# Two attention blocks in one kernel: the second product of layer 0 is copied out of PSUM unscaled and scaled on GpSimd, the prologue is rebuilt, and norms and weight sums are pinned in the instruction order

## The chip, the cores and the metric

One NeuronCore of a Trainium2 chip runs the kernel in a single launch. The metric is the device time in microseconds (us) of one execution. TensorE (PE) does the matrix products, VectorE (DVE), ScalarE (ACT) and GpSimd (POOL) the elementwise work, and SyncE (SP) issues nearly all DMAs. All arithmetic is in float32.

## The reference

Eight images of 512 channels by 32x32 pixels (T = 1024 tokens) pass through two attention layers. Layer 0 has eight heads of 64 channels, layer 1 one head of 512.

```
h   = group_norm(x, 32 groups)                       # layer 0
q, k, v = w_qkv @ h + b_qkv                          # 8 heads, 64 channels each
x   = x + w_proj @ (v softmax(q^T k / 8)) + b_proj
h   = group_norm(x, 8 groups)                        # layer 1
q, k, v = q_w @ h + q_b, k_w @ h + k_b, v_w @ h + v_b
x   = x + p_w @ (v softmax(q^T k / sqrt(512))) + p_b
```

## The kernel before

**Tiling.** An image is four tiles of 128 channels by 1024 tokens (KC = 4). A half is HT = 512 tokens. All 512x512 products of weights and images are done by a Winograd-Strassen scheme with seven half-size products (`wino`, steps 1, 2, 5, 6, 7, 4, 3), so each weight needs three sums and a difference of its quarters (`left_sums`, four VectorE instructions of 128x512 each for a weight in `prepare`, L155 to L158), and each image tile likewise (`right_sums`, L166 to L169). The weight sums are made once, stored in DRAM by `keep`, and read back by `load_weight` for every later image into one of three `wpool` buffers.

**Layer 1 is folded.** Instead of q and k the kernel uses one product matrix m (from the q and k weights), and instead of v and the projection one product matrix z. They are computed on the core in the prologue: `raw` loads a weight, `natural` transposes it on TensorE and copies it out of PSUM, `product` multiplies. `bias_product` multiplies a weight with a bias vector: `ubias` (natural k weight times bq1), `obias[1]` (raw p times bv1, plus bp1) and `obias[0]` (layer 0's projection times bv0, plus bp0). It does this with the weight as the stationary operand and the vector as a moving operand of one column: 16 matmuls for each bias, and a small VectorE instruction per four of them.

**The prologue** in order: load k, q (layer 1), image 0 and the layer 0 weights; transposes of k and q; statistics of image 0; weight sums of v; product m; group mean; `ubias`; the affine terms of the norm; the norm applied to image 0 (two tiles on ScalarE, two on GpSimd); then v, q, k of image 0 by Winograd; the mean of image 1's norm; transposes of v; product z; `obias[1]`, `obias[0]`. After that the loop over the images starts.

**The skewed loop.** For each image b: `attention0(b)`, then the m-product and scores of image b-1's layer 1 and the projection of b's layer 0, the rest of layer 1 of b-1, and q, k, v of b+1.

**`attention0`** is eight blocks (pair of heads hp by token half tb). In each, eight score tiles `sc` go through ScalarE's exponential (L414), VectorE adds the eight results into `sum` (L416, L418), TensorE forms `av` from the exponentials, then `sums` (the column sums of `sum`), of which VectorE takes reciprocals (L378). The reciprocals travel through a DRAM tile `rows` and come back broadcast as `r`. `scaled` multiplies `av` in PSUM by `r` into the result `a` on VectorE (L436); it is called in the next block, between its scores and its `av`. `av` and `sums` share two PSUM buffers (`acc`), the scores have three double ones. `extra` is a list of work given out twice in each block, after the scores and after `av`: in the first image the later weights' sums, in all of them the four `norm.apply` of the next image, on ScalarE (L136).

**Order.** A planner in the framework orders the instructions of each engine by its own estimates. `tc.keep_in_program_order(i)` puts instruction i behind the instruction that was traced just before it on the same engine; what is not so marked may be moved. Before the change only TensorE's instructions are marked. An engine works through its queue in order, so an instruction that waits holds back all behind it on that engine.

Of the kernel before, what the change touches and what calls it, by code (L numbers as in the profile page):

```python
# [15 lines left out]
P = 128  # L16
# [12 lines left out]
def two_attention_blocks_kernel(  # L29
# [35 lines left out]
    def matmul(*args, **kw):  # L65
        tc.keep_in_program_order(nc.tensor.matmul(*args, **kw))  # L66

    def transpose(*args):
        tc.keep_in_program_order(nc.tensor.transpose(*args))
# [5 lines left out]
    def pcol(name, c):  # L75
        return pcols(name)[:, c : c + 1]
# [9 lines left out]


    class GroupNorm:
        def __init__(self, layer, uid):
            self.layer, self.uid = layer, uid  # L90
            self.mv = small.tile([P, KC, 2], F32, tag="mv", name=f"mv_{uid}")
            self.st = [None] * KC

        def half_stats(self, c, half, xh):
            if self.st[c] is None:
                self.st[c] = small.tile([P, 2, 6], F32, tag="bnst", bufs=8, name=f"bnst_{self.uid}_{c}")
            nc.vector.bn_stats(self.st[c][:, half, :], xh)

        def end_stats(self, c):
            nc.vector.bn_aggr(self.mv[:, c, :], self.st[c])  # L100
# [32 lines left out]
        def apply(self, engine, dst, src, c):  # L133
            s, b = self.s[:, c : c + 1], self.b[:, c : c + 1]
            if engine is nc.scalar:
                nc.scalar.activation(dst, src, AF.Identity, bias=b, scale=s)  # L136
            else:
                engine.tensor_scalar(dst, src, s, b, ALU.mult, ALU.add)

# [32 lines left out]
    def main_path(ctx):  # L172
# [14 lines left out]
        def acc_tile(name):  # L187
            return ps_acc.tile([P, HT], F32, tag="acc", name=name)
# [96 lines left out]
        def keep(n, t):  # L285
            nc.sync.dma_start(wdram[n], t)
# [108 lines left out]

        def attention0(b, q, k, v, extra):
            a = channel_tiles(f"a0_{b}")
            scaled = None
            n = 0
            for hp in range(KC):  # L400
                for tb in range(2):
                    uid = f"0_{b}_{hp}_{tb}"
                    total = pair_tile(f"sum_{uid}")
                    es = []
                    for s in range(NS):
                        sc = ps_pools[n % 3].tile([P, 2, HT], F32, tag="sc", name=f"sc_{uid}_{s}")
                        n += 1
                        for j in range(2):
                            matmul(
                                sc[:, j, :], k[hp][ts(j, 64), ts(s, P)], q[hp][ts(j, 64), ts(tb, HT)],  # L410
                                start=True, stop=True,
                            )
                        e = pair_tile(f"e_{uid}_{s}")
                        nc.scalar.activation(e, sc, AF.Exp, scale=(C // 8) ** -0.5)  # L414
                        if s == 1:
                            nc.vector.tensor_add(total, es[0], e)  # L416
                        elif s > 1:
                            nc.vector.tensor_add(total, total, e)  # L418
# [12 lines left out]
                    for f in extra.pop(0) if extra else ():  # L431
                        f()
                    r = reciprocals(total, uid, False)

                    def scaled(hp=hp, tb=tb, av=av, r=r):
                        nc.vector.tensor_mul(a[hp][:, ts(tb, HT)], av, r)  # L436

            assert not extra
            return a, scaled
# [72 lines left out]

        def raw(n, i):
            ts_ = [pair_tile(f"raw{n}_{h}") for h in range(2)]
            for h in range(2):
                nc.sync.dma_start(ts_[h], w[i, ts(h, C // 2), :].rearrange("(kc p) o -> p kc o", p=P))
            return [ts_[kc // 2][:, kc % 2, :] for kc in range(KC)]


        def natural(wt, nm):  # L520
            ts_ = [pair_tile(f"nat{nm}_{h}") for h in range(2)]
            t = [ts_[o // 2][:, o % 2, :] for o in range(KC)]
            for o in range(KC):
                pt = acc_tile(f"tr_w{nm}_{o}")
                for kc in range(KC):
                    transpose(pt[:, ts(kc, P)], wt[kc][:, ts(o, P)], ident)
                if o % 2 == 0:
                    nc.vector.tensor_copy(t[o], pt)
                else:
                    nc.scalar.copy(t[o], pt)  # L530
            return t

        def product(lhs, rhs, nm):
            ts_ = [pair_tile(f"prod{nm}_{h}") for h in range(2)]
            for ic in range(KC):
                ps = acc_tile(f"ps_w{nm}_{ic}")
                for kc in range(KC):
                    matmul(ps, lhs[kc][:, ts(ic, P)], rhs[kc], start=(kc == 0), stop=(kc == KC - 1))
                nc.scalar.copy(ts_[ic // 2][:, ic % 2, :], ps)
            for h in range(2):  # L540
                nc.sync.dma_start(products[nm][ts(h, C // 2), :].rearrange("(kc p) o -> p kc o", p=P), ts_[h])

        def bias_product(dst, lhs, vec, add, nm):
            for oc in range(KC):
                ps = acc_tile(f"ps_b{nm}_{oc}")
                for kc in range(KC):
                    matmul(
                        ps[:, 0:1], lhs[kc][:, ts(oc, P)], pcol(vec, kc), start=(kc == 0), stop=(kc == KC - 1)
                    )
                if add is None:  # L550
                    nc.vector.tensor_copy(dst[:, oc : oc + 1], ps[:, 0:1])
                else:
                    nc.vector.tensor_add(dst[:, oc : oc + 1], ps[:, 0:1], pcol(add, oc))

        def prologue():
            raw_k = raw("k", 5)
            raw_q = raw("q", 4)
            h0 = [load_x(0, c, "h0") for c in range(KC)]
            first = {n: prepare(n) for n in "vqk"}
            wk = natural(raw_k, "k")  # L560
            wq = natural(raw_q, "q")
            norm = GroupNorm(0, "0_0")
            for c in range(KC):
                norm.stats(c, h0[c])
            for f in first["v"][1]:
# [5 lines left out]
            for c in range(KC):  # L571
                norm.apply(nc.scalar if c % 2 else nc.gpsimd, h0[c], h0[c], c)
            raw_v = raw("v", 6)
            raw_p = raw("p", 7)
            hf, steps = image_factors(h0, "h0_0")
            background.extend(steps)
            for n in "qk":
                background.extend(first[n][1])
# [21 lines left out]
            return v, q, k, norm1, later  # L600

        psum_pools("first", 2)
# [360 lines left out]
```

## Time and profile before

| what | value |
|---|---|
| median of 3 timed executions | 2979.69 us (2978.97 to 2979.95) |
| span of the profiled execution | 2980.3 us |
| TensorE busy | 2942.8 us, 99% |
| VectorE busy | 1833.3 us, 62% |
| ScalarE busy | 775.2 us, 26% |
| GpSimd busy | 96.8 us, 3% |
| mean granted TensorE clock | 0.995 |

A line of a group or timeline gives the engine, the line of code, the operation, the tiles written and read, the shapes, and how often; in brackets the idle time of the engine before it and what ended it. All TensorE instructions carry the line of the helper that records them (L66 for matmuls, L69 for transposes), so tiles tell them apart: `ps_wm` and `ps_wz` are the two products, `ps_bu` and `ps_bo` the bias products, `tr_w*` the transposes, `psa_`, `psb_`, `psc_` the Winograd steps. A full float32 matmul of 512 columns shows as two records. The prologue takes 146.5 us of the span; the loop the rest.

### The profile page before, as it was taken

Reading aid. Unit: us, or ns where it says so; the run is one execution under the profiler, and the core shown is the slowest. Engines: PE = TensorE matmul, PEld = TensorE weight load, DVE = VectorE, ACT = ScalarE, POOL = GpSimd, SP = SyncE. Lnnn points to the kernel's source line nnn. Section 1 sums busy time; section 2 is a strip of 40 time slices with the busy share of each in tenths; the row PEclk is TensorE's granted clock in tenths of the full one; section 3 lists DMA queues with packets and bytes.
Section 4 is the critical chain, followed back from the end, with each engine's and each line's share of the span. In section 5 each row is a group of like instructions: output and inputs, shape, how many; then the busy total and the mean of one; then the engine's idle time right before and its main releaser. Section 6 shows DMA issues by size and latency. Waiting matters only on the chain.

```text
span 2980.3 us, 26641 instructions
## 1 busy us (share of the span) xinstructions
PE 2942.8 (99%) x10322; PEld 1408.1 (47%) x10322; DVE 1833.3 (62%) x2443; ACT 775.2 (26%) x941; POOL 96.8 (3%) x105
## 2 busy tenths in 40 slices
PE   7999999999999999999999999999999999999999
PEld 5533533555345453454534545345443455334545
DVE  4377577644776557755577645765467653676555
ACT  1153142112521134111351203411044111531110
POOL 0000000000000000000000000000000000000000
PEclk9999999999999999999999999999999999999999
DMA  6422301132011320223202222122211222112201
GB/s 260 168 80 77 150 16 66 53 145 103 19 64 54 144 106 19 90 79 114 85 20 108 96 74 85 47 82 96 92 71 47 78 103 92 40 43 78 85 7 65
DMA packets 67925, 245.78 MB, mean 82 GB/s; under 512 B 8208, under 2 KB 15184, under 8 KB 61264
## 3 DMA queue, kind: packets, MB, share of 16 engines
q1 hardware_dynamic: 67376, 243.86, 22.4%
q8 instruction: 83, 1.36, 0.2%
q14 instruction: 50, 0.41, 0.0%
q10 hardware_dynamic: 416, 0.16, 0.0%
HBM read 197.03 MB, written 46.96 MB: 82 GB/s over the span
## 4 chain that ended last, share of the span: by engine, by line
PE 85%; DVE 6%; issue 3%; DMA 3%; ACT 2%; SPq 0%; POOL 0%; DVEq 0%; ACTq 0%; POOLq 0%
PE sc L66 9%; PE av L66 9%; PE psb_sc L66 6%; PE psb_av L66 6%; DVE sum L418 5%; PE psa_av L66 4%; PE psa_sc L66 4%; PE psc_av L66 4%; PE psc_sc L66 4%; PE psb_v L66 3%; PE psb_z L66 3%; PE psb_k L66 3%; PE psb_q L66 3%; PE psb_p L66 3%; PE psb_g L66 3%
## 5 line engine op out<-in xcount | busy, mean ns | idle before, releaser
L414 ACT ACTIVATE e<-sc 128x1024 f32<-128x1024 f32 x512 | 477.0, 1049 | 490.2 <-PE sc L66 490.2
L418 DVE TENSOR_TENSOR sum<-sum,e 128x1024 f32<-128x1024 f32 x384 | 470.0, 1224 | 35.9 <-ACT e L414 1.7
L66 PE MATMUL sc<-q,k 64*128 64x512 f32 x2048 | 462.9, 601 | 4.5 <-ACT e L414 4.5
L66 PE MATMUL av<-e,v 128*64 128x512 f32 x2048 | 453.6, 595 | 0.0
L66 PEld LDWEIGHTS sc<-q,k 64*128 64x128 f32 x2048 | 190.0, 187 | 249.8 <-ACT e L414 126.7
L66 PEld LDWEIGHTS av<-e,v 128*64 128x64 f32 x2048 | 141.4, 137 | 304.3 <-issue 285.4
L378 DVE RECIPROCAL rc<-sums 128x256 f32<-128x256 f32 x72 | 126.5, 1756 | 87.3 <-PE sums L66 52.6
L416 DVE TENSOR_TENSOR sum<-e,e 128x1024 f32<-128x1024 f32 x64 | 78.4, 1226 | 69.6 <-ACT e L414 69.6
L465 ACT ACTIVATE e<-e 128x512 f32<-128x512 f32 x96 | 60.6, 631 | 232.2 <-DVE e L464 232.2
L66 PE MATMUL psa_sc<-g,h 128*128 128x512 f32 x256 | 115.7, 594 | 0.0
L66 PE MATMUL psa_av<-e,z 128*128 128x512 f32 x256 | 113.3, 595 | 0.0
L380 POOL TENSOR_TENSOR all_recs<-all_recs,rc 128x256 f32<-128x256 f32 x72 | 64.3, 892 | 1465.2 <-DVE rc L378 1450.7
L136 ACT ACTIVATE h<-h,b,s 128x1024 f32<-128x1024 f32 x62 | 76.4, 1240 | 74.4 <-DMA h<-in_x 51.1
L436 DVE TENSOR_TENSOR a<-av,r 128x512 f32<-128x512 f32 x64 | 44.0, 688 | 62.7 <-DMA r<-rows 62.5
L66 PEld LDWEIGHTS psa_sc<-g,h 128*128 128x128 f32 x256 | 48.1, 190 | 57.9 <-issue 56.2
L66 PEld LDWEIGHTS psa_av<-e,z 128*128 128x128 f32 x256 | 48.0, 190 | 57.3 <-issue 55.9
L245 ACT COPY t_sc<-psa_sc 128x512 f32<-128x512 f32 x32 | 18.7, 586 | 181.7 <-DVE x L640 152.4
L66 PE MATMUL psb_sc<-g,h 128*128 128x512 f32 x128 | 58.1, 597 | 0.0
L66 PE MATMUL psa_z<-w_z,h 128*128 128x256 f32 x256 | 57.9, 379 | 0.0
L66 PE MATMUL psb_z<-w_z,t_h 128*128 128x256 f32 x256 | 57.9, 379 | 0.0
L66 PE MATMUL psa_p<-a,w_p 128*128 128x512 f32 x128 | 57.5, 592 | 0.0
L66 PE MATMUL psb_p<-t_a,w_p 128*128 128x512 f32 x128 | 57.5, 592 | 0.0
(274 smaller groups left out, 3951.5 us busy)
## 6 DMA issues: line engine op xcount, KB each, us to landing
x<-in_x SPq DMA_DIRECT2D x36, 512.0 KB
h<-in_x SPq DMA_DIRECT2D x32, 512.0 KB
r<-rows SPq DMA_DIRECT2D x128, 128.0 KB
spill<-x SPq DMA_DIRECT2D x32, 512.0 KB
h<-spill SPq DMA_DIRECT2D x32, 512.0 KB
x<-spill SPq DMA_DIRECT2D x32, 512.0 KB
out<-x SPq DMA_DIRECT2D x64, 256.0 KB
w_p<-sums_p SPq DMA_DIRECT2D x8, 1792.0 KB
```

The source lines that it names most:

```text
L66: tc.keep_in_program_order(nc.tensor.matmul(*args, **kw))
L136: nc.scalar.activation(dst, src, AF.Identity, bias=b, scale=s)
L245: nc.scalar.copy(t1[i], ps["a", i])
L378: nc.vector.reciprocal(rc, sums)
L380: nc.gpsimd.tensor_tensor(all_recs, all_recs, rc, ALU.add)
L414: nc.scalar.activation(e, sc, AF.Exp, scale=(C // 8) ** -0.5)
L416: nc.vector.tensor_add(total, es[0], e)
L418: nc.vector.tensor_add(total, total, e)
L436: nc.vector.tensor_mul(a[hp][:, ts(tb, HT)], av, r)
L465: nc.scalar.activation(dst, dst, AF.Exp, scale=scale)
```

## The change

It has five parts.

1. **`attention0`**: after `av`, ScalarE copies it unscaled from PSUM to `a`. The multiplication by `r` then runs in place on GpSimd, for all blocks but the last of an image; for that one `scaled` still does it on VectorE, now from SBUF.
2. **Front of the prologue**: `raw` loads in four DMAs of 256 KB instead of two of 512 KB; `natural` transposes into four PSUM buffers of several pools, chunk by chunk in the order of loading, and copies afterwards, VectorE and ScalarE in turn, pinned; the statistics of image 0 are pinned behind those copies; `product` uses the PSUM pool "a" and takes hooks, by which the group mean goes in after matmul 6 of product m, and the affine terms and the norm of image 0 after matmul 9. The weight sums of v come after product m.
3. **`bias_products`**: the three bias vectors are the stationary operand (one column), the weights the moving one (512 columns), three outputs in three row groups of one PSUM bank. The rows are copied to SBUF, sent to DRAM, read back as columns, and added in the first image's attention.
4. **The four sums of each weight in `prepare`** are pinned on VectorE: for p, m, z they stay in blocks 0, 1, 2 of the first image's attention.
5. **`norm.apply` on ScalarE** is pinned.

The core of the diff:

```diff
@@ GroupNorm
-            nc.vector.bn_stats(self.st[c][:, half, :], xh)
+            stats = nc.vector.bn_stats(self.st[c][:, half, :], xh)
+            if self.pinned:
+                tc.keep_in_program_order(stats)
-                nc.scalar.activation(dst, src, AF.Identity, bias=b, scale=s)
+                tc.keep_in_program_order(nc.scalar.activation(dst, src, AF.Identity, bias=b, scale=s))
@@ prepare
-                nc.vector.tensor_add, nc.vector.tensor_sub,
+                lambda *a: tc.keep_in_program_order(nc.vector.tensor_add(*a)),
+                lambda *a: tc.keep_in_program_order(nc.vector.tensor_sub(*a)),
@@ attention0
-                    if scaled:
-                        scaled()
...
+                    dst = a[hp][:, ts(tb, HT)]
+                    nc.scalar.copy(dst, av)
                     r = reciprocals(total, uid, False)
-                    def scaled(hp=hp, tb=tb, av=av, r=r):
-                        nc.vector.tensor_mul(a[hp][:, ts(tb, HT)], av, r)
+                    if (hp, tb) != (KC - 1, 1):
+                        nc.gpsimd.tensor_tensor(dst, dst, r, ALU.mult)
+                    else:
+                        scaled = lambda dst=dst, r=r: nc.vector.tensor_mul(dst, dst, r)
@@ natural
+            pt = [ps_tile(banks[o // 2], f"tr_w{nm}_{o}") for o in range(KC)]
+            for kc in range(KC):
+                for o in range(KC):
+                    transpose(pt[o][:, ts(kc, P)], wt[kc][:, ts(o, P)], ident)
+            spread(lambda o, copy: tc.keep_in_program_order(copy(t[o], pt[o])), KC)
@@ bias_products
+            for kc in range(KC):
+                for i, (m, vec) in enumerate(lhs):
+                    matmul(ps[32 * i : 32 * i + 1, :], pcol(vec, kc), m[kc], start=(kc == 0), stop=(kc == KC - 1))
...
+            nc.sync.dma_start(rows, row[0 : 32 * n : 32, :C])
...
+                nc.sync.dma_start(cols[:, i, :], rows[i].rearrange("(c p) -> p c", p=P))
@@ prologue
-            product(wq, wk, "m")
-            norm.group_mean(acc_tile("gmean_0_0")[:, :KC])
-            bias_product(ubias, wk, "bq1", None, "u")
-            norm.affine(acc_tile("gvar_0_0")[:, :KC])
...
+            product(
+                wq, wk, "m", {6: lambda: norm.group_mean(acc_tile("gmean_0_0")[:, :KC]), 9: normed},
+            )
...
-            product(natural(raw_v, "v"), raw_p, "z")
-            bias_product(obias[1], raw_p, "bv1", "bp1", "o")
-            bias_product(obias[0], raw("p0", 3), "bv0", "bp0", "o0")
+            raw_p0 = raw("p0", 3)
+            wv = natural(raw_v, "v", "bc")
+            product(wv, raw_p, "z")
+            bias = bias_products([(wk, "bq1"), (raw_p, "bv1"), (raw_p0, "bv0")])
...
+            later.append([
+                lambda: tc.keep_in_program_order(nc.vector.tensor_copy(ubias, bias[0])),
+                lambda: tc.keep_in_program_order(nc.vector.tensor_add(obias[1], bias[1], pcols("bp1"))),
+                lambda: tc.keep_in_program_order(nc.vector.tensor_add(obias[0], bias[2], pcols("bp0"))),
+            ])
```

More of the change, by code (lines that the diff above doesn't have):

```diff
@@ L88, in two_attention_blocks_kernel, with __init__ @@
     class GroupNorm:
-        def __init__(self, layer, uid):
-            self.layer, self.uid = layer, uid
+        def __init__(self, layer, uid, pinned=False):
+            self.layer, self.uid, self.pinned = layer, uid, pinned
             self.mv = small.tile([P, KC, 2], F32, tag="mv", name=f"mv_{uid}")
@@ L397, in attention0 @@
             a = channel_tiles(f"a0_{b}")
-            scaled = None
             n = 0
@@ L514, in raw, with ps_tile @@
             ts_ = [pair_tile(f"raw{n}_{h}") for h in range(2)]
-            for h in range(2):
-                nc.sync.dma_start(ts_[h], w[i, ts(h, C // 2), :].rearrange("(kc p) o -> p kc o", p=P))
+            for kc in range(KC):
+                nc.sync.dma_start(ts_[kc // 2][:, kc % 2, :], w[i, ts(kc, P), :])
             return [ts_[kc // 2][:, kc % 2, :] for kc in range(KC)]
-        def natural(wt, nm):
+        def ps_tile(n, name):
+            return acc_tile(name) if n == "acc" else ps_pools["abc".index(n)].tile([P, HT], F32, tag="ps", name=name)
@@ L521, in natural, with spread @@
+        def spread(f, n):
+            for i in range(n):
+                f(i, nc.scalar.copy if i % 2 else nc.vector.tensor_copy)
+        def natural(wt, nm, banks):
             ts_ = [pair_tile(f"nat{nm}_{h}") for h in range(2)]
             t = [ts_[o // 2][:, o % 2, :] for o in range(KC)]
[L523 to L530, printed above, removed]
@@ L531, in natural, with product @@
-            return t
-        def product(lhs, rhs, nm):
+            pt = [ps_tile(banks[o // 2], f"tr_w{nm}_{o}") for o in range(KC)]
[3 more added lines that the diff above has]
+            spread(lambda o, copy: tc.keep_in_program_order(copy(t[o], pt[o])), KC)
+            return t
+        def product(lhs, rhs, nm, hooks=()):
+            hooks = dict(hooks)
             ts_ = [pair_tile(f"prod{nm}_{h}") for h in range(2)]
@@ L535, in product @@
             for ic in range(KC):
-                ps = acc_tile(f"ps_w{nm}_{ic}")
+                ps = ps_tile("a", f"ps_w{nm}_{ic}")
                 for kc in range(KC):
                     matmul(ps, lhs[kc][:, ts(ic, P)], rhs[kc], start=(kc == 0), stop=(kc == KC - 1))
+                    if ic * KC + kc in hooks:
+                        hooks[ic * KC + kc]()
                 nc.scalar.copy(ts_[ic // 2][:, ic % 2, :], ps)
-            for h in range(2):
-                nc.sync.dma_start(products[nm][ts(h, C // 2), :].rearrange("(kc p) o -> p kc o", p=P), ts_[h])
@@ L543, in bias_product @@
[L543 to L548, printed above, removed]
-                    )
[L550 to L553, printed above, removed]
+                if ic % 2:
+                    nc.sync.dma_start(
+                        products[nm][ts(ic // 2, C // 2), :].rearrange("(kc p) o -> p kc o", p=P), ts_[ic // 2]
+                    )
@@ new lines, in bias_products @@
+        def bias_products(lhs):
+            n = len(lhs)
+            ps = acc_tile("ps_bias")
+            for kc in range(KC):
+                for i, (m, vec) in enumerate(lhs):
+                    matmul(ps[32 * i : 32 * i + 1, :], pcol(vec, kc), m[kc], start=(kc == 0), stop=(kc == KC - 1))
+            row = big_tile("bias_rows")
+            rows = dram.tile([n, C], F32, name="bias_rows_dram")
+            for i in range(n):
+                nc.vector.tensor_copy(row[32 * i : 32 * i + 1, :C], ps[32 * i : 32 * i + 1, :])
+            nc.sync.dma_start(rows, row[0 : 32 * n : 32, :C])
+            cols = const.tile([P, n, KC], F32, name="bias_cols")
+            for i in range(n):
+                nc.sync.dma_start(cols[:, i, :], rows[i].rearrange("(c p) -> p c", p=P))
+            return [cols[:, i, :] for i in range(n)]
@@ L559, in prologue, with normed @@
             first = {n: prepare(n) for n in "vqk"}
-            wk = natural(raw_k, "k")
-            wq = natural(raw_q, "q")
-            norm = GroupNorm(0, "0_0")
+            wk = natural(raw_k, "k", ("a", "b"))
+            wq = natural(raw_q, "q", ("c", "acc"))
+            norm = GroupNorm(0, "0_0", pinned=True)
             for c in range(KC):
                 norm.stats(c, h0[c])
+            hf, steps = image_factors(h0, "h0_0")
+            def normed():
+                norm.affine(acc_tile("gvar_0_0")[:, :KC])
+                for c in range(KC):
+                    norm.apply(nc.scalar if c % 2 else nc.gpsimd, h0[c], h0[c], c)
+            product(
+                wq, wk, "m", {6: lambda: norm.group_mean(acc_tile("gmean_0_0")[:, :KC]), 9: normed},
+            )
+            raw_v = raw("v", 6)
+            raw_p = raw("p", 7)
             for f in first["v"][1]:
                 f()
-            product(wq, wk, "m")
-            norm.group_mean(acc_tile("gmean_0_0")[:, :KC])
-            bias_product(ubias, wk, "bq1", None, "u")
-            norm.affine(acc_tile("gvar_0_0")[:, :KC])
[L571 to L575, printed above, removed]
             background.extend(steps)
```

## The prediction

> **What bounds the kernel now.** First the page's busy table: TensorE is busy 99% of the span, so only three things can move the end: TensorE's idle time, work that TensorE need not do, and time at a low clock. I then asked for all of TensorE's waits.
>
> ```profile
> PE sums L66 <- DVE sum L418: 10.1, 23, 1.4
> PE tr_wk L69 <- DMA rawk<-in_w: 5.9, 2, 5.0
> PE sc L66 <- ACT e L414: 4.5, 7, 0.7
> PE tr_wk L69 <- DVE natk L528: 4.4, 1, 4.4
> PE psa_v L66 <- POOL h L138: 3.3, 1, 3.3
> ```
>
> (columns: us in total, times, longest). In the loop TensorE waits only at `sums` and `sc`: 14.6 us. Everything else is in the prologue, which TensorE's timeline shows next.
>
> ```profile
> 4.99 0.66 PE L69 MATMUL tr_wk<-ident,rawk 128*128 128x128 f32 x2 [4.99 <-DMA rawk<-in_w]
> 12.49 1.97 PE L69 MATMUL tr_wk<-ident,rawk 128*128 128x128 f32 x8 [4.36 <-DVE natk L528]
> 16.94 1.10 PE L69 MATMUL tr_wq<-ident,rawq 128*128 128x128 f32 x8 [0.68 <-ACT natq L530]
> ...
> 119.20 14.00 PE L66 MATMUL ps_wz<-rawp,natv 128*128 128x512 f32 x32
> 133.57 1.05 PE L66 MATMUL ps_bo<-par,rawp 128*128 128x1 f32 x8 [0.26 <-DVE ve L123]
> 134.93 11.60 PE L66 MATMUL ps_bo<-par,rawp 128*128 128x1 f32 x56 [0.31 <-DVE obias L553]
> 146.47 10.15 PE L66 MATMUL sc<-q,k 64*128 64x512 f32 x32
> ```
>
> Two things to see. One-column matmuls of `obias` hold TensorE from 133.57 to 146.47, 12.9 us. And the first block's scores take 10.15 us where every later block's take 7.14. The windows around them say why (after the stretch: its length, busy time and count of PE, PEld, DVE, ACT and POOL, the granted clock, the DMA share and GB/s):
>
> ```profile
> 136.00:146.00 10.00, 10.00 (x49) 10.00 (x48) 0.95 (x6) 2.45 (x2) 0.00 (x0) 0.50 1.04 393
> 146.00:152.00 6.00, 6.00 (x17) 2.90 (x19) 3.26 (x6) 2.67 (x3) 0.00 (x0) 0.50 1.00 425
> 152.00:156.00 4.00, 4.00 (x18) 1.60 (x18) 3.08 (x3) 4.00 (x5) 0.00 (x0) 0.93 0.95 407
> ```
>
> The clock is halved some 2.2 us after the one-column matmuls begin and is back only at about 152.3. The same happens once earlier: `ubias` and the wait for the norm halve it at 36.5, until 46.6, into v's first steps.
>
> **What the Trainium skill says.** (1) "TensorE: Matmul & The Clock Gate", What's actually happening: an idle window of about 3.4 us halves the array's clock, a busy one restores it. The trace agrees, with one addition: dense one-column matmuls are treated like idleness. (2) "TensorEngine Tiling (Array Packing)", Theoretical Speedup: stationary operands of at most 32 columns run up to four at a time. Agreed: `sums`, four matmuls in four column groups, takes 0.57 us from its start to the next `sc`, where one after another would be 4 x 0.43 = 1.7. (3) "SBUF — State Buffer", Who interferes with whom: a VectorE instruction with two SBUF inputs and a GpSimd instruction that reads SBUF exclude each other for the whole instruction. The trace fits: while GpSimd normed a tile (L138, 1.70 us instead of 1.20) VectorE's `t_h` took 1.52 us instead of 0.69. (4) Price: "GPSIMD Engine Reference", Elementwise: a two-input add of 2048 columns 4.50 us, so an estimate of 1.1 us for 512.
>
> **The front of the prologue (part 2).** Now v's first matmul is at 40.82. The transposes stop after six of k because VectorE, in order, sits on the statistics until image data lands (10.35), and its copy of `natk` comes behind them at 11.79. After: each engine has both copies in order before any statistics, and four PSUM buffers per weight, so transposes follow the loads. k's 1 MB had landed by 6.58; at the 0.40 to 0.43 MB per us of the next windows q's 1 MB lands about 9.1. Last four transposes 1.0 us (eight took 1.97), then on each engine two copies in a row, 0.69 each on VectorE, of which the first matmuls need one and the third and fourth the other: product m starts about 11.3 instead of 18.39. It runs 14.0, plus 0.3 for two small mean matmuls: end 25.6. The norm must keep up: statistics from 11.6, eight of 0.64 and four of 0.20, are done by about 17.3 (image tile 3 lands by about 14.3); matmul 6 ends at 11.3 + 7 x 0.86 = 17.3, so no more than 0.5 of wait; the mean's four small VectorE steps 0.8; matmul 9 at about 20.3; ve to b, on the trace 37.59 to 39.46, is 1.9: 22.3; the first tiles from GpSimd and ScalarE 1.25 later, 23.6. This lies beside the product. v then needs only the copies out of pool "a", the last two behind the norms on ScalarE: 0.6. v starts at about 26.3, **14.5 us earlier** (bounds 10 to 16.5). `ubias`'s 4.3 us on TensorE are in this sum. VectorE's weight sums of v (4 x 0.69 from 22.3) and the image sums (8 x 0.69) end before 33, where step 5 of v needs them (26.3 + 6.9). More SP issues (8 loads for 4, about 0.48 each) put q's last issue at 4.6, before its data could land; image and weight loads shift by 2 us within a DMA stream that is full anyhow. The weight sums of q, k come later than at 21 to 26, but are needed after 50.
>
> Without a pause before v the clock stays up: 40.8 to 46.6 at half speed is **2.9 us** saved (0 to 2.9).
>
> **From k to the first attention (part 3).** After: group mean as now; 16 transposes (2.0), up to 0.7 of wait for the last read of `psc_k` (117.0), first copy 0.69: product z starts at 119.5 instead of 119.2 in old time, ends with the variance matmul at 133.6. Then 12 matmuls of 512 columns, 0.86 each alone; in three column groups four rounds of 0.86, 3.6 with the fill. Neither width 1 nor this packing is in the trace: from below 3.4, from above 12 x 0.86 = 10.3 (no overlap). I take 3.6, since `sums` packs. End 137.2 instead of 146.47: **9.3 us** (2.6 to 9.5). Rows, the DRAM trip and its 4-byte columns: nothing, since the biases are first read at the projection, over 100 us later; the three tiny adds sit in block 3's VectorE slack.
>
> The 512-column stream should count as busy, and 3.6 us is short: the clock stays, the first block takes 7.1 instead of 10.1: **3.0 us** (0 to 3.0).
>
> **Attention (parts 1, 4, 5).** In a quiet block VectorE's adds end before `sums` is due; in one out of two or three the multiplication waits for `r` in VectorE's queue and the adds behind it are late:
>
> ```profile
> 403.00 0.69 DVE L436 TENSOR_TENSOR a<-av,r 128x512 f32<-128x512 f32 x1 [1.89 <-DMA r<-rows]
> 403.61 6.53 DVE L418 TENSOR_TENSOR sum<-sum,e 128x1024 f32<-128x1024 f32 x5
> 410.96 1.76 DVE L378 RECIPROCAL rc<-sums 128x256 f32<-128x256 f32 x1 [0.82 <-PE sums L66]
> ```
>
> That queue wait leaves VectorE for GpSimd, which has nothing behind it but `all_recs`. VectorE's block is then 9.2 (adds, first start to last end) after a first start 3.2 behind the scores' start: done at 12.4 of the 14.1 at which `sums` is due, 1.7 us free. GpSimd's multiplication excludes VectorE's adds for 1.1 (price above) up to 1.8 (twice `all_recs`, 0.89 for half the columns, of which some is waiting). The lower value fits into 1.7 and I take it; the upper leaves 0.1 per block, 6 us in all. ScalarE's copy (0.59 as `natk`) comes at the end of `av`, when ScalarE idles about 7 us; the next exponential is due 1.4 later, the PSUM buffer 7.6 later: nothing. The pinned norms go behind a block's exponentials, where ScalarE is idle; that removes the 0.65 us at the start of seven attentions (TensorE at `sc` behind an early L136). The pinned weight sums, 2.76 in each of blocks 0 to 2 of the first image, follow the adds and delay the reciprocal by about 1.2, of which the next block's first add feels 0.4; their stores and reloads are due at 250 or later. Of the 14.6 us I count **12.5** (0 to 14.6; below nothing is the last rival).
>
> **Sum.** 14.5 + 2.9 + 9.3 + 3.0 + 12.5 = 42.2; span 2980.3 - 42.2 = 2938.1. The timed median is 0.6 below the profiled span: 2937.5, so **2938**.
>
> **Rivals.** *A, the bias matmuls do not overlap or look idle to the clock gate*: 6.7 us more, or 3.0, or both: 2941 to 2948. For it: one-column operands did trip the gate. Against: they were the moving ones. *B, the VectorE/GpSimd exclusion eats the attention gain*: adds late by about 0.2 in most blocks, 12 us: about 2950. For: the stretched L138. Against: 1.7 us of slack. *C, the front stays bound by loads and statistics*: v at 30 to 31, clock dip kept: 2945. *D, slower*: same mechanism as B, but GpSimd holds the port longer. Prologue and `sc` gains are 34.2; over 63 blocks a wait of 0.54 each on top of the present 0.16 (10.1 / 63) undoes them, so GpSimd would have to hold VectorE off for 1.7 + 0.7 = 2.4 us per block; at 3.0 us it is 2980 + 63 x 0.6 = 3018. Against: it is twice the price.
>
> **Chances.** Likeliest 0.60, A 0.14, B 0.10, C 0.11, D 0.05. Likeliest's own range is 2931 to 2944; with A, C and most of B the range is 2930 to 2951. Less than 0.2% (6 us) can't be told from no change: faster 0.93, same 0.02, slower 0.05.
>
> **What would show it.** Product m starting near 11, v near 26; no low clock from 26 on nor at the first attention; a `ps_bias` group of about 3.6 us; TensorE's waits at `sums` and `sc` near zero; GpSimd's new multiplication at 1.1 to 1.8 us. Wrong would be `sums` waiting on `sum` in most blocks, or ScalarE's copy queued behind the next exponentials.

## The result and the profile after

The changed kernel takes 2934.85 us (median of 4 executions, 2933.78 to 2936.12) against 2979.82 before: ratio 0.9848, 95% interval 0.9831 to 0.9865. The forecast was 2938 (2930 to 2951), faster. The profiled execution has a span of 2934.3, 46.0 less than the 2980.3 of before.

The page's first lines and the group lines that answer to those read before (after the bar: busy us and mean ns; then idle time ahead of the group, and who ended it):

```profile
span 2934.3 us, 26701 instructions
PE 2919.7 (100%) x10250; PEld 1390.3 (47%) x10250; DVE 1852.9 (63%) x2381; ACT 809.3 (28%) x1005; POOL 201.7 (7%) x161
...
L421 DVE TENSOR_TENSOR sum<-sum,e 128x1024 f32<-128x1024 f32 x384 | 519.3, 1352 | 41.4 <-DVE sum L421 0.9
...
L435 ACT COPY a<-av 128x512 f32<-128x512 f32 x64 | 37.5, 586 | 321.3 <-PE av L66 321.3
...
L438 POOL TENSOR_TENSOR a<-a,r 128x512 f32<-128x512 f32 x56 | 104.0, 1857 | 276.1 <-DMA r<-rows 260.0
```

GpSimd has taken the multiplication over and does the waiting for `r` (260 us in sum, harmless there). VectorE's adds have become longer, 1352 instead of 1224 ns. TensorE's waits (us in total, times, longest; the three others are 0.5 or less each):

```profile
PE tr_wk L69 <- DMA rawk<-in_w: 4.6, 2, 3.7
PE psb_q L66 <- DVE u_q L237: 1.2, 1, 1.2
PE psb_v L66 <- DVE w_v L237: 0.5, 1, 0.5
```

The waits at `sums` and `sc` are gone, and two that were not there have come: `u_q`, 1.2 us, and `w_v`, 0.5 us. TensorE's timeline through the prologue:

```profile
8.80 3.29 PE L69 MATMUL tr_wq<-ident,rawq 128*128 128x128 f32 x16
12.55 6.28 PE L66 MATMUL ps_wm<-natk,natq 128*128 128x512 f32 x14 [0.46 <-DVE natq L539]
18.81 0.36 PE L66 MATMUL gmean<-mv,gm 128*128 128x4 f32 x2
...
27.06 7.07 PE L66 MATMUL psa_v<-prepare_v,h 128*128 128x256 f32 x32
...
103.25 13.97 PE L66 MATMUL ps_wz<-rawp,natv 128*128 128x512 f32 x32 [0.50 <-ACT natv L539]
117.06 0.28 PE L66 MATMUL gvar<-dv,gm 128*128 128x4 f32 x2
117.27 0.59 PE L66 MATMUL ps_bias<-natk,par 128*1 128x512 f32 x1
117.27 0.60 PE L66 MATMUL ps_bias<-rawp,par 128*1 128x512 f32 x2
...
120.80 7.14 PE L66 MATMUL sc<-q,k 64*128 64x512 f32 x32
127.87 7.09 PE L66 MATMUL av<-e,v 128*64 128x512 f32 x32
```

Between the variance matmul and the first scores lie now 3.5 us of `ps_bias` instead of 12.9, and these scores take 7.14 at once. The windows give a clock of 1.00 through the whole prologue. For its first 11.6 us that is no measurement, since the trace has no clock record there, and the transposes in that time are slow (see e8); from 11.6 us on the clock is at 1.00. From the first TensorE instruction of each stage in both timelines:

| stage | before | after | gain | forecast |
|---|---|---|---|---|
| start to v of image 0 | 40.8 | 27.1 | 13.8 | 14.5 |
| v of image 0 | 27.2 | 25.0 | 2.2 | 2.9 |
| q, k of image 0 | 48.1 | 48.1 | 0.0 | 0 |
| mean of image 1 to first attention | 30.4 | 20.7 | 9.7 | 9.3 |
| attention of image 0 | 121.2 | 117.2 | 3.9 | 3.0 and a share of the next but one |
| from there to attention 1 | 97.4 | 98.9 | -1.5 | 0 |
| attention of images 1 to 7 | 839.2 | 820.6 | 18.6 | 12.5 with image 0's share |
| all else | | | -0.7 | 0 |

Every one of the 64 blocks of attention now takes what the shortest took before: 7.07 for scores, 7.02 for `av`, 0.57 for `sums`. Before, the starts show 10.6 us above that at scores (3.0 of it by the clock in the first block, 1.08 in the first block of each later image) and 11.8 at `av` and the wait behind it.

### The profile page after: what moved, and what is told of

It is laid out like the page before. It is cut to its first block, busy times and chain, and to the rows that moved or that the text cites. A ratio compares the mean times of both kernels' runs of the same rounds, so it can differ in the third digit from the quotient of the medians.

```text
span 2934.3 us, 26701 instructions
## 1 busy us (share of the span) xinstructions
PE 2919.7 (100%) x10250; PEld 1390.3 (47%) x10250; DVE 1852.9 (63%) x2381; ACT 809.3 (28%) x1005; POOL 201.7 (7%) x161
## 4 chain that ended last, share of the span: by engine, by line
PE 98%; DVE 1%; DMA 0%; issue 0%; ACT 0%; SPq 0%; DVEq 0%
PE sc L66 15%; PE av L66 15%; PE psb_sc L66 6%; PE psb_av L66 6%; PE psa_av L66 4%; PE psa_sc L66 4%; PE psc_av L66 4%; PE psc_sc L66 4%; PE psb_z L66 3%; PE psb_g L66 3%; PE psb_k L66 3%; PE psb_p L66 3%; PE psb_v L66 3%; PE psb_q L66 3%; PE psa_g L66 2%; PE psa_v L66 2%
## 5 line engine op out<-in xcount | busy, mean ns | idle before, releaser
L421 DVE TENSOR_TENSOR sum<-sum,e 128x1024 f32<-128x1024 f32 x384 | 519.3, 1352 | 41.4 <-DVE sum L421 0.9
L66 PE MATMUL sc<-q,k 64*128 64x512 f32 x2048 | 456.8, 596 | 0.0
L435 ACT COPY a<-av 128x512 f32<-128x512 f32 x64 | 37.5, 586 | 321.3 <-PE av L66 321.3
L438 POOL TENSOR_TENSOR a<-a,r 128x512 f32<-128x512 f32 x56 | 104.0, 1857 | 276.1 <-DMA r<-rows 260.0
L127 POOL TENSOR_TENSOR rstd<-ve,mhalf 128x4 f32<-128x4 f32 x16 | 16.3, 1019 | 1204.1 <-DVE ve L125 1204.1
L66 PEld LDWEIGHTS psa_sc<-g,h 128*128 128x128 f32 x256 | 48.1, 190 | 57.9 <-issue 56.2
L248 ACT COPY t_sc<-psa_sc 128x512 f32<-128x512 f32 x32 | 18.7, 586 | 181.7 <-DVE x L669 152.4
```

Source lines behind the costliest of these rows:

```text
L127: nc.gpsimd.tensor_tensor(rstd, ve, mhalf, ALU.pow)
L248: nc.scalar.copy(t1[i], ps["a", i])
L435: nc.scalar.copy(dst, av)
L438: nc.gpsimd.tensor_tensor(dst, dst, r, ALU.mult)
```

## The experiments

Unless said otherwise each is the changed kernel with one thing altered. Chips differ: the kernel before took 2979.65 beside e1 to e4, 2975.74 beside e5 to e8, 2979.04 beside e9 to e12. The changed kernel run once more beside e9 to e12 gave 2933.74, the number that I subtract; beside e5 to e8, where the kernel before was 3 us quicker, it was not run, so their differences may be up to some 3 us larger. Part 2 is the one part that no run undoes by itself.

### e11: the changed kernel again

> The changed kernel unaltered, beside the others of this job on the same chip. All theories: about 2935, ratio 0.985. It also shows how far the start of product m scatters from run to run (12.5 in the first profile, 10.5 to 11.8 in the experiments with the same front).

Measured: 2933.74 (2933.09 to 2935.11), ratio 0.9847 (0.9834 to 0.9861). Product m started at 11.76. Over the profiles of kernels with the same front (the first one, e1 to e5, e7, e9, e11) this start lies between 10.4 and 12.6: the front scatters by 2 us.

### e1: part 3 undone

```diff
+        def bias_product(dst, lhs, vec, add, nm):     # as in the kernel before
...
-            bias = bias_products([(wk, "bq1"), (raw_p, "bv1"), (raw_p0, "bv0")])
+            bias_product(ubias, wk, "bq1", None, "u")
+            bias_product(obias[1], raw_p, "bv1", "bp1", "o")
+            bias_product(obias[0], raw_p0, "bv0", "bp0", "o0")
```

> The changed kernel with part 3 undone: the three biases again with the weight stationary and one-column moving operands, 48 small products after product z. Theory of the prediction: TensorE takes about 17.3 us for them (one bias 4.3 at full clock, two at half clock 6.5 each) instead of 3.5, and the halved clock costs the first attention block 3.0 more: 2935 + 16.8 = about 2952, first block of scores 10.1 us. Rival: the clock has nothing to do with these products but with the time at which image 1's norm and loads run; then the first block stays at 7.1 us and the clock at 1.0, and only the 4.3 x 3 - 3.5 = 9.4 are lost: about 2944.

Measured: 2949.57 (2948.03 to 2952.78), 15.8 more. TensorE's timeline and the windows of e1 (PE, PEld, DVE, ACT and POOL busy, then granted clock, DMA share, GB/s):

```profile
115.64 3.98 PE L66 MATMUL ps_bu<-par,natk 128*128 128x1 f32 x32
119.48 13.79 PE L66 MATMUL ps_bo<-par,rawp 128*128 128x1 f32 x64
133.20 10.20 PE L66 MATMUL sc<-q,k 64*128 64x512 f32 x32
```

```profile
120.00:133.00 13.00, 13.00 (x63) 13.00 (x62) 1.11 (x7) 0.00 (x0) 0.00 (x0) 0.50 0.38 141
133.00:139.00 6.00, 6.00 (x16) 2.73 (x17) 1.07 (x2) 2.31 (x3) 0.00 (x0) 0.50 0.00 0
```

17.6 us for the products instead of 3.5, the clock halved from 118.9, which is 3.3 us after they begin, until 139.4, through most of the first block, and 3.1 us lost there. TensorE is busy without a gap all that time, so idleness in the sense of the timeline is not what halves the clock. The rival, that the loads around it did, does not fit: DMA is idle in the second window, and in the changed kernel it is busy for 0.91 of 117 to 121 us at a clock of 1.00.

### e2: three bias rows in one column group

```diff
-                    matmul(ps[32 * i : 32 * i + 1, :], pcol(vec, kc), m[kc], ...)
+                    matmul(pss[i][0:1, :], pcol(vec, kc), m[kc], ...)     # pss: three PSUM banks
```

In the changed kernel the three results are rows 0, 32 and 64 of one bank, so in three column groups; here each is row 0 of its own bank, all in one group.

> The changed kernel with the three bias rows all in row 0 of three different PSUM banks, so that all twelve one-column stationary operands share one column group. Theory (packing is what makes them cheap): twelve in a row at 0.86, 10.3 us instead of 3.5: about 2942, clock still 1.0 since the 512-column stream counts as busy. Rival 1 (a one-column operand is quick in any group): 2935. Rival 2 (a single used column looks idle to the clock gate and only the short duration saved it): half clock after some 3 us, 17 us for the products and 3 us in the first block: about 2952.

Measured: 2941.68 (2940.67 to 2941.93), 7.9 more. Each of the twelve takes its 0.86:

```profile
115.49 1.02 PE L66 MATMUL ps_biasb<-natk,par 128*1 128x512 f32 x2
116.35 1.02 PE L66 MATMUL ps_biasc<-rawp,par 128*1 128x512 f32 x2
117.21 1.02 PE L66 MATMUL ps_biasa<-rawp,par 128*1 128x512 f32 x2
...
126.82 7.14 PE L66 MATMUL sc<-q,k 64*128 64x512 f32 x32 [0.86 <-DVE bias_rows L568]
```

10.3 us instead of 3.5, and 0.9 of wait for a PSUM bank that my edit borrowed. The packing in column groups is worth 6.8 us. The windows over these 10 us, read as in e1, show a clock of 1.00:

```profile
115.00:121.00 6.00, 6.00 (x17) 1.33 (x16) 0.65 (x4) 0.58 (x1) 1.01 (x1) 1.00 0.39 139
121.00:127.00 6.00, 5.14 (x14) 1.05 (x14) 2.04 (x3) 0.00 (x0) 0.00 (x0) 1.00 0.13 43
```

A 512-column stream through one used column keeps the clock up; a one-column stream through 128 used columns (e1) does not.

### e4: part 1 undone

```diff
-                    nc.scalar.copy(dst, av)
                     r = reciprocals(total, uid, False)
-                    if (hp, tb) != (KC - 1, 1):
-                        nc.gpsimd.tensor_tensor(dst, dst, r, ALU.mult)
-                    else:
...
+                    scaled = lambda dst=dst, r=r, av=av: nc.vector.tensor_mul(dst, av, r)   # called in the next block
```

> The changed kernel with part 1 undone as a whole: VectorE multiplies av from PSUM by r in the next block, no copy on ScalarE. Both readings: the 11.8 us that the av stages took over their shortest in the kernel before come back, about 2946 to 2947; the first blocks of scores stay at 7.1, since part 5 is kept. Rival (part 1 did nothing and part 5 all of it): 2935.

Measured: 2955.2 (2954.08 to 2956.63), 21.5 more, some 9 beyond the forecast. Images 1 to 7 lose 10.7 us in attention, about what they lost before. The other 11.0 are in image 0, where `r` comes late:

```profile
149.41 0.69 DVE L439 TENSOR_TENSOR a<-av,r 128x512 f32<-128x512 f32 x1 [3.64 <-DMA r<-rows]
150.01 1.22 DVE L422 TENSOR_TENSOR sum<-sum,e 128x1024 f32<-128x1024 f32 x1
151.15 0.69 DVE L284 TENSOR_TENSOR prepare_m<-prepare_m 128x512 f32<-128x512 f32 x1
```

Here the pinned weight sums stand behind the multiplication: parts 1 and 4 touch. With the wait on VectorE, 2.6 us of pinned sums come on top of it in three blocks. Of the 11.0, 1.7 are a halved clock: 0.50 from 170.5 to 174.0, after a wait of 3.7 us at `sums`.

### e3 and e9: the multiplication back on VectorE, from SBUF, at two places

e3 keeps ScalarE's copy and gives the multiplication to VectorE, called as in the kernel before. e9 is e3 with that instruction pinned:

```diff
-                        nc.gpsimd.tensor_tensor(dst, dst, r, ALU.mult)
...
+                    scaled = lambda ...: nc.vector.tensor_mul(dst, dst, r)                            # e3
+                    scaled = lambda ...: tc.keep_in_program_order(nc.vector.tensor_mul(dst, dst, r))  # e9
```

> The changed kernel with ScalarE's copy kept, but the multiplication by r again on VectorE, from SBUF, called where it was before. Separates two readings of part 1. Queue theory (the prediction's: what cost time was VectorE waiting for r with the adds behind it): TensorE's waits for the sum return, 10 to 12 us in the loop: about 2946. Buffer theory (what cost time was av's PSUM buffer held until r came): the copy alone cures it: 2935, no waits at sums.

> As e3 (ScalarE copies av, VectorE multiplies by r from SBUF), but the multiplication is pinned behind the adds of the next block, where r has long landed; e3's planner had put it behind the second add, and VectorE waited there for r in nearly every block. Queue theory: with nothing to wait for, 0.69 us more VectorE work fits into what is free in a block, and the time is that of the changed kernel again, 2935 plus or minus 3, with no waits at sums outside image 0. Rival (VectorE has no room for this work at all, which is why GpSimd must take it): waits at sums remain, 2950 or more.

Measured: e3 2977.46 (2974.71 to 2981.08), 43.7 more, nearly the kernel before. e9 2932.68 (2932.19 to 2933.05), the changed kernel's time. VectorE's timeline of one block in e3, then in e9:

```profile
731.64 1.23 DVE L422 TENSOR_TENSOR sum<-sum,e 128x1024 f32<-128x1024 f32 x1
734.34 0.69 DVE L440 TENSOR_TENSOR a<-a,r 128x512 f32<-128x512 f32 x1 [1.48 <-DMA r<-rows]
734.95 6.54 DVE L422 TENSOR_TENSOR sum<-sum,e 128x1024 f32<-128x1024 f32 x5
742.25 1.76 DVE L382 RECIPROCAL rc<-sums 128x256 f32<-128x256 f32 x1 [0.76 <-PE sums L66]
```

```profile
741.56 7.87 DVE L422 TENSOR_TENSOR sum<-sum,e 128x1024 f32<-128x1024 f32 x6
749.35 0.68 DVE L440 TENSOR_TENSOR a<-a,r 128x512 f32<-128x512 f32 x1
751.93 1.76 DVE L382 RECIPROCAL rc<-sums 128x256 f32<-128x256 f32 x1 [1.90 <-issue]
```

The instructions are the same; their place is not. In e3 the planner set the multiplication behind the second add, `r` is not there, and five adds wait 1.5 us behind it; TensorE then waited for `sum` 54 times, 30.9 us. In the kernel before and in e4 only about every second block has the multiplication there (the others have it behind the sixth add, where outside image 0 it waits for nothing), and TensorE waited 23 times; that is why e3 loses more than e4. In e9 it stands behind the last add, waits for nothing, and 1.9 us remain. The buffer reading (the copy alone cures it) is refuted by e3, the reading that VectorE has no room by e9. What cost time was the wait for `r` inside VectorE's queue, and GpSimd is one of two ways to take it out. That the copy is what allows so late a place (without it `av`'s PSUM buffer would be held until the end of the next block's adds) is argued, not tried.

### e5: part 5 undone

```diff
-                tc.keep_in_program_order(nc.scalar.activation(dst, src, AF.Identity, bias=b, scale=s))
+                nc.scalar.activation(dst, src, AF.Identity, bias=b, scale=s)
```

> The changed kernel with part 5 undone: the norms on ScalarE are not pinned. Theory: the planner puts one of them between the first exponentials of an attention again, the first scores of seven attentions take 8.15 instead of 7.07 us: 7.6 us more, about 2942.5. Rival (the first blocks became quick because VectorE and ScalarE had less else to do): 2935.

Measured: 2952.39 (2952.02 to 2952.49), ratio 0.992 (0.9904 to 0.9937), 18.7 more. Seven times 1.08 in the first blocks, 7.6 us, are as expected. The other 11.3 are in the very first block; 8.5 of them are a wait of TensorE and some 2.7 a clock halved behind it (0.50 from 126.3 to 133.1). On ScalarE:

```profile
121.13 1.24 ACT L139 ACTIVATE h<-h,b,s 128x1024 f32<-128x1024 f32 x1 [5.38 <-DMA h<-in_x]
127.90 1.24 ACT L139 ACTIVATE h<-h,b,s 128x1024 f32<-128x1024 f32 x1 [5.53 <-DMA h<-in_x]
129.04 1.92 ACT L417 ACTIVATE e<-sc 128x1024 f32<-128x1024 f32 x2
```

and on TensorE:

```profile
118.71 2.85 PE L66 MATMUL sc<-q,k 64*128 64x512 f32 x12
130.10 4.33 PE L66 MATMUL sc<-q,k 64*128 64x512 f32 x12 [8.54 <-ACT e L417]
```

The planner sets two norms of image 1 ahead of the first exponential. In the kernel before their data landed at 138.9 while TensorE was still at `obias` until 146.5, so the same place cost nothing there. With attention starting at 118.7 the loads are not done, and all exponentials wait behind the norms.

### e6: part 4 undone

```diff
-                lambda *a: tc.keep_in_program_order(nc.vector.tensor_add(*a)),
-                lambda *a: tc.keep_in_program_order(nc.vector.tensor_sub(*a)),
+                nc.vector.tensor_add, nc.vector.tensor_sub,
```

> The changed kernel with part 4 undone: the four sums of each weight in the preparation are not pinned. Theory: they lie beside TensorE's work wherever they stand: 2935 plus or minus 1.5; VectorE's sums of k no longer stand before w_v in v of image 0, which gives back 0.5. Rival: without the pin the planner puts them ahead of the statistics and the norm of image 0 and the front is 3 to 6 us later: 2938 to 2941.

Measured: 2947.83 (2945.8 to 2948.5), ratio 0.9904 (0.9887 to 0.992), 14.1 more, and outside both expectations. The rival's 3 to 6 us in the front are there: v's sums go between the statistics of image 0 and wait for their load, the mean is 2.4 us late, the clock is halved from 19.4 to 22.8, which costs 1.5 more, and v of image 0 starts 19.0 after the start of product m instead of 14.5. The rest, 9.5, is in the first attention:

```profile
132.18 0.69 DVE L158 TENSOR_TENSOR prepare_z<-prepare_z 128x512 f32<-128x512 f32 x1 [7.13 <-DMA prepare_z<-product_z]
...
134.72 1.22 DVE L418 TENSOR_TENSOR sum<-e,e 128x1024 f32<-128x1024 f32 x1
```

VectorE waits for product z to come back from DRAM, with the adds of the first block behind it, and `sums` is 7.0 late; the clock, halved from 142.3 to 149.1, costs the other 2.4. Again a wait that the slow bias products used to cover.

### e10: parts 2 and 3 alone

This is e4, e5 and e6 in one: the new prologue with the old attention, norms and weight sums.

> Parts 2 and 3 alone: the rebuilt prologue, with attention, norms and weight sums as before (part 1, 4 and 5 undone). If the parts are independent, as the prediction added them: 2980 - 26 - 3 = about 2951. Theory formed from e5 and e6: a prologue that ends 26 us sooner opens two new waits in the first attention, ScalarE in its queue for image 1's loads (11 us in e5) and VectorE for product z's reload (7 us in e6, and 4 us in the front): about 2965 to 2972.

Measured: 2968.7 (2966.31 to 2970.14), ratio 0.9963 (0.995 to 0.9976). A prologue that brings the first attention 23.3 us forward (123.1 instead of 146.5) is worth only some 10 us by itself: the first attention then takes 134.0 us where the kernel before took 121.2. ScalarE waits 11.6 and 3.4 us for loads ahead of the first exponentials, VectorE 7.8 us for `prepare_z`, at the same time, and the clock is halved from 129.2 to 142.9. The parts do not add.

### e7: GpSimd's multiplication twice

```diff
+                        nc.gpsimd.tensor_tensor(again, dst, r, ALU.mult)
                         nc.gpsimd.tensor_tensor(dst, dst, r, ALU.mult)
```

> The changed kernel with GpSimd's multiplication done twice per block, once into a scratch tile. One multiplication stretched VectorE's adds by 0.9 us a block and left 1.55 us before sums is due. Exclusion theory: two stretch them by 1.8 to 2.5, so the adds come 0.3 to 0.9 late in 56 blocks: 2950 to 2985. Rival (GpSimd's second instruction finds its place in the time in which VectorE is idle or in instructions with one SBUF input): 2935, adds at most 1.5 us longer.

Measured: 2948.21 (2946.03 to 2950.39), ratio 0.9906 (0.989 to 0.9923), some 14 to 15 more. The groups of e7:

```profile
L422 DVE TENSOR_TENSOR sum<-sum,e 128x1024 f32<-128x1024 f32 x384 | 566.2, 1474 | 41.4 <-DVE sum L422 0.9 <-ACT e L418 0.5 <-DVE sum L420 0.5
L440 POOL TENSOR_TENSOR a<-a,r 128x512 f32<-128x512 f32 x56 | 117.4, 2096 | 4.4
L439 POOL TENSOR_TENSOR again<-a,r 128x512 f32<-128x512 f32 x56 | 107.9, 1927 | 266.6 <-DMA r<-rows 180.1 <-PE sc L66 51.2 <-ACT e L418 23.7
```

Per add 1224, 1352, 1474 ns with no, one and two multiplications on GpSimd: each costs VectorE's adds the same, 47 to 49 us in all. ScalarE's copy is not the cause: in e9, which has it too, an add takes 1225 ns. The expectation's 1.55 us of free time was too much. From the last add's end to `sums` it is 1.7 us in 61 blocks of e9, 0.8 in 42 of the changed kernel's and 0.05 in 53 of e7's. So one multiplication fits and two do not: 10.3 us are lost at `av` and `sums`, and 3.4 more between the attentions.

How the two engines meet is seen on single instructions of the changed kernel, two cases:

```profile
402.68 1.23 DVE L421 TENSOR_TENSOR sum<-sum,e 128x1024 f32<-128x1024 f32 x1
402.69 2.35 POOL L438 TENSOR_TENSOR a<-a,r 128x512 f32<-128x512 f32 x1 [4.16 <-DMA r<-rows]
404.01 2.12 DVE L421 TENSOR_TENSOR sum<-sum,e 128x1024 f32<-128x1024 f32 x1
...
733.05 1.28 POOL L438 TENSOR_TENSOR a<-a,r 128x512 f32<-128x512 f32 x1 [4.18 <-DMA r<-rows]
733.07 2.34 DVE L421 TENSOR_TENSOR sum<-sum,e 128x1024 f32<-128x1024 f32 x1
```

In the first an add runs already: it keeps its 1.2 us, the multiplication takes 2.35 instead of its shortest 1.27, and the next add waits in turn. In the second the multiplication is ahead and keeps its time, and the add takes 1.1 us longer. Of the 56 multiplications 53 meet these adds, and each of them makes one add 0.9 to 1.1 us longer; the three that meet a reciprocal make no add longer. This agrees with the Trainium skill, "SBUF — State Buffer", Who interferes with whom, that a VectorE instruction with two SBUF inputs and a GpSimd instruction that reads SBUF exclude each other.

### e8 and e12: the clock in the front

e8 adds six matmuls of a tile of ones ahead of the transposes; their result is not read. e12 also moves VectorE's sums of k out of v of image 0.

```diff
+            warm = acc_tile("warm")
+            for i in range(6):
+                matmul(warm[:, :P], ones, ones, start=True, stop=True)
```

> The changed kernel with six more 128-column matmuls of a tile of ones ahead of the first transposes, into a PSUM tile that nothing reads. Theory: the transposes of q run at the low clock (16 in 3.3 us) and hold product m back to 12.5; with TensorE busy from 1.1 us on the clock is up by the time k's second half lands, product m starts about 11.2: 1.2 us less, about 2933.7. Rival (the loads set the start of product m): no change.

> e8's six matmuls ahead of the transposes, and VectorE's sums of layer 0's k weight moved out of v into q of image 0, which takes away the 0.5 us that TensorE waited for w_v. Theory: with product m at about 10.2 and no wait in v, 1 to 2.5 us less than the unaltered kernel beside it: 2932.5 to 2934. Rival: scatter of the front hides it: no change within 1 us.

Measured: e8 2932.78 (2931.85 to 2933.48), ratio 0.9856 (0.9839 to 0.9872); e12 2932.94 (2932.46 to 2933.01) beside e11's 2933.74. Product m starts at 10.2 and 10.8; without these matmuls it was 10.4 to 12.6. The wait for `w_v` is gone in e12. All five executions of e12 lie below the five of e11, by 0.8 us in the median, but the ratios' intervals are nearly the same (0.9831 to 0.9858 against 0.9834 to 0.9861): whether it beats the changed kernel is not shown. The 0.8 is short of the 1 to 2.5 that e12 was expected to gain; e8's 1.0 compares two chips.

What the traces do show is where the scatter of the front comes from. The transposes of q, first in the changed kernel, then in e9, which has the same front (ns of one: shortest, median, longest; then the first and last start):

```profile
L69 PE MATMUL tr_wq<-ident,rawq x16: 272/421/421, 8.8 to 11.8; 128*128 128x128 f32 x16
L69 PE MATMUL tr_wq<-ident,rawq x16: 272/273/328, 7.3 to 9.7; 128*128 128x128 f32 x16
```

The transposes begin slow, about 421 ns each, and become quick, 272. In all fourteen profiles this happens within 0.2 us of the start of the trace's first clock record, which is one of full clock: at 6.7 (e9) to 11.6 us (the changed kernel) with the same front, at 4.8 and 4.7 in e8 and e12. So the theory of e8 holds for the transposes: the six matmuls bring the full clock earlier. But once they are quick the loads hold product m: in e8, e9 and e12 the transposes of q wait 1.0 to 1.1 us for `rawq`, and no product m starts before 10.2.

## Why the prediction was right, point by point

**Front of the prologue**: 13.8 for 14.5. The order was right; that it is the cause is read from the two timelines, since no run undoes part 2 alone. Product m started at 12.55, not 11.3, and the term that failed is that of the transposes: the prediction let them keep up with the loads, with four of q left when its last data land at 9.1. But they ran slow until the clock came up at 11.6: eight of k from 6.97 took 2.04, and the sixteen of q, from 8.80, took 3.29. In the other executions of the same front the clock came up earlier and product m started at 10.4 to 11.8, so how near the forecast came here is in part chance. (The prediction reads six transposes of k before the stop; its own lines show 2 + 6, eight. Nothing hangs on it.)

**Clock**: as predicted in both places. v gained 2.2 for 2.9, since some 0.7 went to the new wait for `w_v` (0.5 in the list of waits, the rest in the timeline around it), behind the pinned sums of k: the step "the weight sums of q, k come later" was costed at nothing and was not quite free. The first block gained the 3.0 in full.

**Bias products**: 3.5 for 3.6. e1 and e2 show both halves, duration and clock, and that packing makes the duration.

**Attention**: 12.5 was too small. The excess of block times over their shortest shows 19.4 besides the clock (7.6 at the first scores, 11.8 at `av` and behind), all gained. The step that failed is "of the 14.6 us I count 12.5". The 14.6 came from the list of waits, which shows 0.65 of the 1.08 at a first block (the rest sits in a matmul's record or behind it). And the 2.1 us between 12.5 and 14.6, for which the prediction gives no term, were gained too: the adds grew by 0.9 per block, which left 0.8 of its 1.7 us free in most blocks. Rival B and rival D fall with this; e7 puts two multiplications, not one, past the edge.

**New wait**: 1.5 us were lost in q of image 1, which I did not foresee. VectorE waits there for the last block's `r`, with the sums of `a` and then `u_q` behind it:

```profile
248.24 0.69 DVE L440 TENSOR_TENSOR a<-a,r 128x512 f32<-128x512 f32 x1 [4.33 <-DMA r<-rows]
...
252.47 0.68 DVE L237 TENSOR_TENSOR u_q<-psb_q,t_q 128x512 f32<-128x512 f32 x1
```

The same wait was 3.24 before, and TensorE did not feel it. In e1, e4, e8 and e9 TensorE does not wait there either, and e1 and e8 have the same loop; what decides the 1.1 us more of `r` stays open.

**The pins (parts 4 and 5)**: here the reasoning was wrong though the sum was not. I costed part 4 at nothing and part 5 at up to 4.5 us at `sc`. Undone, they cost 14.1 and 18.7. The step that failed is to take their worth from the waits of the kernel before. Before, the planner's early places were harmless because TensorE was late anyway; the prologue part removes that cover, and without the pins and part 1 gives back most of its gain (e10: 2968.7 where the sum of parts gives 2951). The four parts undone one by one (3, 1, 4, 5: 15.8, 21.5, 14.1, 18.7) come to 70, far above the 45 of the whole. That the forecast held in this point is luck: the pins went in together with the prologue, and the prediction had no term for the waits that they keep away.

**Rival A** (no overlap or a low clock) and **C** (front bound by loads) did not happen.

## What to carry to other kernels

When a stage is shortened, ask of each engine what stands in its queue at the stage's end that was waiting for a DMA under the old cover: in e5, e6 and e10 it was these waits that came out, on ScalarE and VectorE, when TensorE's prologue had become shorter. An instruction whose input comes by DMA belongs in the queue behind the work that does not need it; where it stands can be worth more than which engine does it (e3 and e9, 45 us apart). To size what a loop can gain, take each stage's excess over its own shortest, not the list of waits alone: here the list showed 14.6 of 19.4 us.

## What the runs showed of the hardware beyond what was expected

- What halves TensorE's clock is not idle time alone: gapless one-column moving operands do (0.50 from 3.3 us after they begin in e1), while 10 us of 512-column streams through a single used column leave it at 1.00 (e2).
- A long wait of TensorE can cost more than itself: behind waits of 8.5 (e5), 7.0 (e6) and 3.7 us (e4) the clock was halved for 6.8, 6.8 and 3.4 us, which cost 2.7, 2.4 and 1.7 us more. A wait of 2.4 us was followed by a halved clock in e6 (at 19.4) and not in e4 (at 151.3).
- GpSimd's two-input multiplication of 128x512 (1.27 us at its shortest) and VectorE's two-input adds of 128x1024 (1.22 us) took turns: in 53 of 53 meetings one add became 0.9 to 1.1 us longer, and where the add was first, the multiplication too (up to 2.35). Beside a reciprocal, which has one input, the multiplication at 180.25 us kept its 1.27 and the reciprocal its 1.76.
- The start of the first product scatters by 2 us between executions with the same front. Their first clock record, of full clock, began between 6.7 and 11.6 us; before it a transpose took about 421 ns, after it 272, and 16 of them from 2.48 to 3.29 us.
